# Preparing the attention's weights behind the norms instead of at the head of the expert walk

## The chip, the cores and the metric

The kernel runs on one core of a Trainium2 chip. A core has a TensorE (PE, matmul; its weight loads are listed as PEld), a VectorE (DVE), a ScalarE (ACT), a GpSimd (POOL) and a SyncE (SP, which here issues DMAs). Each engine works through its own list of instructions in order; engines wait for each other by semaphores. The metric is the time of one execution on the device in microseconds (us). The clock times below count from the start of the profiled span.

## The reference

The input x has 2 x 1024 rows of 256. Every row is normalized; the result xn goes to two branches whose outputs are added to x.

```
xn = layernorm(x)
out = x + attention(xn) + moe(xn)

attention: tokens of 16 channels (each row of 256 holds 16 of them), on a grid of 256 x 64
  q, k, v = tok @ qkv_w
  two branches of 8 channels: softmax attention inside windows of 8 tokens (1 x 8 and 8 x 1),
  plus a depthwise 3 x 3 convolution of v with its bias
  att = concat(branches) @ proj_w + proj_b
  tok + layernorm(att) * ln_w + ln_b

moe: 16 experts with 176 hidden units, plus a shared expert with 352
  scores = sigmoid(xn @ gate.T); of 4 groups of experts the best 2, of those the best 6 experts
  out = sum over the chosen experts of weight * (silu(xn @ gate_e.T) * (xn @ up_e.T)) @ down_e.T
        + shared expert
```

A convolution over a window that is one token wide uses only three of the nine taps, so the whole path from xn to the convolution's share of the attention output is linear. The kernel folds it into small matrices once per call.

## The kernel before

**Norms.** x lies in 128 partitions, 16 rows in each, as four groups of four. `statistics(g)` and `normalized(g)` make means, scales and normalized rows of a group; PE transposes them (L244) into xnT, copied out by ACT (L247) and DVE (L249). `logits(g)` makes the routing's logits (L255, L260).

**Shared expert.** `meanwhile(until)` lays steps of the shared expert between the other work by a budget: products pg and pu (L273), Silu on ACT (L281), the gated product on DVE (L282, tile room), the down product py (L288), the copy to ysh (L289), and after each group of four an accumulating store of ysh to the output, issued by POOL (L291).

**Routing.** From L343 to L538 DVE finds groups, experts and ranks, sorts the 2048 rows by expert sets into 16 tiles of 128, and makes the lists. Its scratch tile tmp holds eight pieces of 128 x 256.

**Walk.** `sorted_tile(t)` gathers a tile's rows (POOL, L817, three buffers), transposes them (px, L821), copies them (xsT, L822) and their weights (wsrt, L824). For each tile three units of two experts follow, and some extra units. `begun` makes the up products pr_u (L853), Silu (L855) and hms on DVE (L856); `hidden` transposes hms (ph, L867) and copies (hT, L869); `finished` makes the down products pr_y (L879) and gives the sum to a scatter that adds into the output (L994). Over the slots the planner lays steps of the attention: `while step and done[0] <= pace * done[1]`, where done sums up estimated costs of DVE and PE and pace comes from in_walk, the estimated costs of all steps. Other small jobs (`extras_listed` at L546, `lists_begun` at L900) are laid into fixed slots.

**Attention.** Four heads (two halves of the batch, two halves of the row). `project(i)` makes pq (L671) from wq and copies q, k and v on ACT (L673 to L676), `products` and `scores` (L684, L688), `highest` (L694 to L696), `weighted` and `values` (L705, L710), `divide` (L718), and `transposed` (L725, L727) into oT. At the end `attended` (L761) adds the projection wp and the folded convolution lp with the bias pbc (pp, L777), normalizes, and the result is stored by accumulation.

**The part that is moved.** `weights_prepared` makes wq, wp, lp and pbc from the weights that DMAs brought at the start. Its steps are qp8 (L583), pqp and qprep (L586, L588), wq (L592), the centring of prep and pb (L598 to L600), wp, rd and wvr (L605 to L612), pm, pb and mm (L615 to L621), ppb and pbc (L626 to L628), and lp (L633 to L642). Before, `all_steps` yields eight of these, each with an estimate of 1.0 for DVE and 0.1 for PE, ahead of the attention's steps.

What decides the final order: a scheduling layer takes the kernel's recorded instructions and lays them out engine by engine; it may move an instruction ahead of others that were recorded earlier where its inputs allow. In the profiled kernel qp8 and the two wvr copies run at 18.6 to 21.8 us, among the norms.

Buffers that tie these parts together: the tag qk holds the routing's tmp and later the attention's q and k; ysum and ysh share the tag ysum; the two PSUM buffers of ps_m (tag m) serve the transposes of the norms, pqp, pm, ppb, px, pq and po; the tag xd holds qp8, wvr, pb8, part and pair_i (two buffers).

Of the kernel before, what the change touches and what calls it, by code (L numbers as in the profile page):

```python
# [8 lines left out]
F32 = mybir.dt.float32  # L9
# [4 lines left out]
ALU = mybir.AluOpType  # L14
AX = mybir.AxisListType
# [7 lines left out]
P = 128  # L23
B, H, W = 2, 1024, 256
C = 16
# [26 lines left out]
def csw_block_moe(ctx: ExitStack, tc: tile.TileContext, x, qkv_w, conv_w0, conv_b0, conv_w1, conv_b1,  # L52
# [58 lines left out]
    ident = const.tile([P, P], F32, name="ident")  # L111
# [89 lines left out]
    cbc = const.tile([C, 1], F32, name="cbc")  # L201
# [4 lines left out]
    band = const.tile([P, 3, 8], F32, name="band")  # L206
# [108 lines left out]
    def meanwhile(until):  # L315

        while spent[1] is not None and spent[0] + spent[1] <= until:
            spent[0] += spent[1]
            spent[1] = next(share)

    held = statistics(0)
    for g in range(4):
        now, held = held, statistics(g + 1) if g < 3 else None
        normalized(g, *now)
        if g > 0:
            logits(g - 1)
        meanwhile((0, 3.4, 6.8, 6.8)[g])
    table_of(AF.Sigmoid, xnT[:, 0, 15, P - 1 : P])
    logits(3)

# [124 lines left out]
    for c in range(15, -1, -1):  # L455
# [3 lines left out]
        to = beats[:, 0:n].rearrange("p c q -> p (c q)")  # L459
# [33 lines left out]
    for n in range(2):  # L493
        nc.vector.tensor_tensor(ohp[:, 8 * n : 8 * n + 8], row_h.unsqueeze(1).to_broadcast(wide),
                                place[:, 1, 8 * n : 8 * n + 8].unsqueeze(2).to_broadcast(wide), ALU.is_equal)
        for c in range(8 * n, 8 * n + 8):
# [38 lines left out]
                     start=True, stop=True)  # L535
# [10 lines left out]
    def extras_listed():  # L546
# [24 lines left out]
        nc.vector.tensor_scalar(xrow[:, 1], xrow[:, 1], NX, None, op0=ALU.add)  # L571
        nc.vector.tensor_scalar(xrow[:, 2], xrow[:, 2], 4, None, op0=ALU.logical_shift_right)
        yield


    def weights_prepared():

        qp8 = work.tile([4 * C, 8, C], F32, tag="xd", name="qp8", bufs=2)
        nc.vector.tensor_copy(qp8, qpT.unsqueeze(1).to_broadcast([4 * C, 8, C]))  # L583
        yield
        pqp = ps_m.tile([P, 4 * C], F32, tag="m", name="pqp")
        nc.tensor.transpose(pqp, qp8.rearrange("k t c -> k (t c)"), ident[0 : 4 * C, 0 : 4 * C])  # L586
        qprep = const.tile([P, 4 * C], F32, name="qprep")
        nc.vector.tensor_copy(qprep, pqp)  # L588
        yield
        qrep, prep = qprep[:, 0 : 3 * C], qprep[:, 3 * C : 4 * C]  # L590
        for s in range(3):
            nc.vector.tensor_tensor(wq[:, s], qrep[:, C * s : C * s + C].unsqueeze(1).to_broadcast([P, 8, C]),  # L592
                                    band[:, 0, :].unsqueeze(2).to_broadcast([P, 8, C]), ALU.mult)
        yield

        def centred(v):
            m = small.tile([P, 1], F32, tag="cm", name="cm")
            nc.vector.tensor_reduce(out=m, in_=v, axis=AX.X, op=ALU.add)  # L598
            nc.vector.tensor_scalar(m, m, 1.0 / C, None, op0=ALU.mult)
            nc.vector.tensor_scalar(v, v, m, None, op0=ALU.subtract)  # L600

        centred(prep)
        centred(pb)
        yield
        nc.vector.tensor_tensor(wp, prep.unsqueeze(1).to_broadcast([P, 8, C]),  # L605
                                band[:, 0, :].unsqueeze(2).to_broadcast([P, 8, C]), ALU.mult)
        rd = const.tile([C, 5, C], F32, name="rd")
        nc.vector.tensor_tensor(rd, prep[0:C, :].unsqueeze(1).to_broadcast([C, 5, C]),
                                tp.unsqueeze(2).to_broadcast([C, 5, C]), ALU.mult)
        wvr = work.tile([C, 2, 8, C], F32, tag="xd", name="wvr", bufs=2)  # L610
        nc.vector.tensor_copy(wvr[:, 0], wvT.unsqueeze(1).to_broadcast([C, 8, C]))
        nc.vector.tensor_copy(wvr[:, 1].rearrange("p t c -> p (t c)"), cbc.to_broadcast([C, P]))  # L612
        yield
        pm = ps_m.tile([P, 6, C], F32, tag="m", name="pm")
        nc.tensor.matmul(pm[:, 0:5, :].rearrange("p d c -> p (d c)"), lhsT=wvr[:, 0].rearrange("p t c -> p (t c)"),  # L615
                         rhs=rd.rearrange("p d c -> p (d c)"), start=True, stop=True)
        nc.tensor.matmul(pm[:, 5, :], lhsT=wvr[:, 1].rearrange("p t c -> p (t c)"), rhs=prep[0:C, :], start=True,
                         stop=True)
        nc.vector.tensor_tensor(pb, pb, pm[:, 5, :], ALU.add)
        mm = const.tile([P, 5, C], F32, name="mm")  # L620
        nc.vector.tensor_copy(mm, pm[:, 0:5, :])  # L621
        yield

        ppb = ps_m.tile([P, P], F32, tag="m", name="ppb")
        pb8 = work.tile([P, 8, C], F32, tag="xd", name="pb8", bufs=2)
        nc.vector.tensor_copy(pb8, pb.unsqueeze(1).to_broadcast([P, 8, C]))  # L626
        nc.tensor.transpose(ppb, pb8.rearrange("p t c -> p (t c)"), ident)
        nc.vector.tensor_copy(pbc, ppb[:, 0:1])  # L628
        yield
        part = work.tile([P, 2, 8, C], F32, tag="xd", name="part", bufs=2)  # L630

        def banded(to, tap, d):
            nc.vector.tensor_tensor(to, mm[:, tap, :].unsqueeze(1).to_broadcast([P, 8, C]),  # L633
                                    band[:, d, :].unsqueeze(2).to_broadcast([P, 8, C]), ALU.mult)

        banded(lp[:, 0], 1, 0)
        banded(part[:, 0], 0, 1)
        banded(part[:, 1], 2, 2)
        banded(lp[:, 1], 3, 0)
        banded(lp[:, 2], 4, 0)  # L640
        nc.vector.tensor_tensor(lp[:, 0], lp[:, 0], part[:, 0], ALU.add)
        nc.vector.tensor_tensor(lp[:, 0], lp[:, 0], part[:, 1], ALU.add)  # L642
        yield

    wq = const.tile([P, 3, 8, C], F32, name="wq")
    wp = const.tile([P, 8, C], F32, name="wp")
    lp = const.tile([P, 3, 8, C], F32, name="lp")
    pbc = const.tile([P, 1], F32, name="pbc")


    oT = big.tile([P, 4, 2, 4, P], F32, name="oT", tag="oT")
# [392 lines left out]

    att = []

    def all_steps():
        for _ in weights_prepared():
            yield 1.0, 0.1, lambda: None
        yield from attention_steps()  # L1050

    def attention_steps():
        for b in range(B):
            for h in range(2):
                yield from attention(b, h)
# [16 lines left out]
    of_slot = {"six": (0.5, 2.0), "extra": (0.8, 2.5)}  # L1072
    of_tile = (0.75, 0.25)
    END = 72
    in_walk = [8 * 1.0 + 4 * (16 * 2.3 + 3.3 + 2.5 + 1.5 + 1.4) + 0.6 + 8 * 1.4, 8 * 0.1 + 4 * 6.2 + 8 * 3.9]
    done = [0.0, 0.0]
    whole = [in_walk[n] + NTL * TOPK * of_slot["six"][n] + NL * of_slot["extra"][n] + NTL * of_tile[n] for n in range(2)]
    pace = (whole[0] - END * of_slot["six"][0] / of_slot["six"][1]) / (whole[1] - END)
# [1 line left out]
    def counted(cost):  # L1080
        for n in range(2):
            done[n] += cost[n]

    walk = all_steps()
    sorted_tile(0)
    meanwhile(100)
    sorted_tile(1)
# [50 lines left out]
    with tc.For_i(0, count_, 1) as n:  # L1138
# [3 lines left out]
        to = small.tile([P, 1], I32, tag="to", name="to")  # L1142
# [60 lines left out]
```

## Time and profile before

| what | value |
|---|---|
| median of 3 runs | 447.4 us (447.02 to 449.18) |
| profiled execution | 447.97 us |
| its span, first to last instruction | 446.3 us |
| mean granted clock of TensorE | 0.987 |
| qprep (L588) of the preparation | 102.15 us |
| last addition of lp (L642) | 111.79 us |
| first product of the attention (L684) | 119.05 us |
| landing of a ysh store, shortest, median, longest | 5.4, 5.6, 7.9 us |

The profile lists, for an instruction or a group, its start, its duration, and in brackets the idle time of its engine just before it with what ended that idle time. A wait for several semaphores is put down to the one that came last by the profile. The chain of waits follows the end back to the start, step by step to what released each.

### The profile page before, as it was taken

Reading aid. Unit: us, or ns where it says so; the run is one execution under the profiler, and the core shown is the slowest. Engines: PE = TensorE matmul, PEld = TensorE weight load, DVE = VectorE, ACT = ScalarE, POOL = GpSimd, SP = SyncE. Lnnn points to the kernel's source line nnn. Section 1 sums busy time; section 2 is a strip of 40 time slices with the busy share of each in tenths; the row PEclk is TensorE's granted clock in tenths of the full one; section 3 lists DMA queues with packets and bytes.
Section 4 is the critical chain, followed back from the end, with each engine's and each line's share of the span. In section 5 each row is a group of like instructions: output and inputs, shape, how many; then the busy total and the mean of one; then the engine's idle time right before and its main releaser. Section 6 shows DMA issues by size and latency. Waiting matters only on the chain.

```text
span 446.3 us, 6293 instructions
## 1 busy us (share of the span) xinstructions
PE 393.4 (88%) x1668; PEld 246.3 (55%) x1669; DVE 291.5 (65%) x515; ACT 214.1 (48%) x535; POOL 197.9 (44%) x207
## 2 busy tenths in 40 slices
PE   0999999997899788998897999999998899979990
PEld 0435465664466555565564666656665555446670
DVE  4624958635699979289995999959999223322210
ACT  2945258322544442643635456364533657774320
POOL 7300000314273299457524245615554274779432
PEclk9999999999999999999999999999999999998997
DMA  8999941324023101101212124210332101822922
GB/s 232 338 304 321 275 154 30 64 67 86 25 71 73 32 25 34 29 23 33 38 39 60 35 43 81 47 36 24 69 90 56 22 14 57 103 68 74 126 44 24
DMA packets 40178, 37.56 MB, mean 84 GB/s; under 512 B 5300, under 2 KB 37616, under 8 KB 40112
## 3 DMA queue, kind: packets, MB, share of 16 engines
q0 software_dynamic: 11616, 13.52, 18.4%
q1 hardware_dynamic: 27472, 22.59, 16.4%
q10 hardware_dynamic: 1056, 1.05, 0.7%
q8 instruction: 15, 0.25, 0.2%
q14 instruction: 19, 0.16, 0.1%
HBM read 27.70 MB, written 12.45 MB: 90 GB/s over the span
## 4 chain that ended last, share of the span: by engine, by line
DVE 38%; PE 30%; DMA 10%; issue 8%; ACT 7%; POOL 5%; DVEq 0%; POOLq 0%; ACTq 0%; SPq 0%
DVE s L688 6%; PE pr_u L853 6%; DVE pv L705 6%; DVE pr L684 5%; DVE o L710 5%; DVE hms L856 5%; PE pp L777 4%; PE pq L671 3%; PE pr_y L879 3%; DMA out_dram<-ysum,lists 3%; PE pg L273 3%; PE py L288 2%; DMA xg<-xw_d,lists 2%; PE pu L273 2%; DMA xx<-in_x_dram 2%
## 5 line engine op out<-in xcount | busy, mean ns | idle before, releaser
L853 PE MATMUL pr_u<-w1s,xsT 128*128 x384 | 128.4, 468 | 3.4 <-DVE hms L856 2.4
L853 PEld LDWEIGHTS pr_u<-w1s,xsT 128*128 128x128 f32 x384 | 69.9, 191 | 39.4 <-issue 7.7
L994 POOL DMA_INDIRECT out_dram<-ysum,lists x30 | 57.2, 1908 | 77.4 <-ACT ysum L1040 20.3
L855 ACT ACTIVATE sg<-pr_u 128x176 f32<-128x176 f32 x110 | 34.7, 317 | 77.1 <-PE pr_u L853 70.2
L856 DVE SCALAR_TENSOR_TENSOR hms<-sg,w,pr_u 128x176 f32<-128x176 f32 x96 | 36.8, 387 | 35.5 <-ACT sg L855 35.5
L684 DVE TENSOR_TENSOR pr<-qk 128x2048 f32<-128x2048 f32 x16 | 36.6, 2288 | 17.6 <-ACT qk L673 17.2
L705 DVE TENSOR_TENSOR pv<-s,v 128x2048 f32<-128x2048 f32 x16 | 36.5, 2284 | 2.5 <-ACT s L696 2.4
L867 PE MATMUL ph<-ident,hms 128*128 128x128 f32 x165 | 31.7, 282 | 5.5 <-DVE hms L856 2.9
L688 DVE TENSOR_REDUCE s<-pr 128x256 f32<-128x2048 f32 x16 | 36.5, 2279 | 0.1
L955 POOL TENSOR_SCALAR ysum<-row_h,spot 128x128 f16<-128x128 f16 x26 | 28.0, 1094 | 19.2 <-PE rows_of L946 14.9
L710 DVE TENSOR_REDUCE o<-pv 128x256 f32<-128x2048 f32 x16 | 36.3, 2269 | 0.0
L980 POOL DMA_INDIRECT xg<-xw_d,lists x14 | 21.6, 1540 | 29.3 <-DVE hms L856 15.5
L867 PEld LDWEIGHTS ph<-ident,hms 128*128 128x128 f32 x165 | 21.5, 144 | 23.2 <-DVE hms L856 6.9
L291 POOL DMA_DIRECT2D out_dram<-ysh x4 | 3.7, 928 | 64.5 <-ACT ysh L289 64.5
L817 POOL DMA_INDIRECT xg<-xw_d,lists x16 | 19.8, 1239 | 25.4 <-PE ph L867 9.3
L879 PE MATMUL pr_y<-w2a,hT 128*128 x96 | 29.1, 386 | 0.0
L879 PE MATMUL pr_y<-wts,hT 128*128 128x256 f32 x96 | 29.0, 384 | 0.0
L879 PE MATMUL pr_y<-w2b,hT 112*128 x96 | 28.8, 381 | 0.0
L671 PE MATMUL pq<-wq,rows 128*128 128x384 f32 x64 | 25.1, 506 | 3.3 <-ACT oT L727 1.9
L869 ACT COPY hT<-ph 128x384 f32<-128x384 f32 x55 | 26.4, 480 | 2.8 <-PE ph L867 1.8
L853 PE MATMUL pr_u<-w1s,xd 128*128 x56 | 20.4, 487 | 6.6 <-ACT xd L989 6.6
L288 PE MATMUL py<-room 128*128 128x256 f32 x96 | 23.9, 387 | 0.7 <-DVE room L282 0.7
(403 smaller groups left out, 712.2 us busy)
## 6 DMA issues: line engine op xcount, KB each, us to landing
w1s<-in_w_dram SPq DMA_DIRECT2D x22, 256.0 KB, 4.4
wts<-in_w_dram SPq DMA_DIRECT2D x55, 64.0 KB, 2.1
wts<-in_w_dram SPq DMA_DIRECT2D x55, 48.0 KB, 1.7
xw_d<-xx SPq DMA_DIRECT2D x4, 544.0 KB, 4.6
w2a<-in_w_dram SPq DMA_DIRECT2D x4, 512.0 KB, 9.4
out_dram<-ysh POOLq DMA_DIRECT2D x4, 512.0 KB, 5.6
xr<-xw_d POOLq DMA_DIRECT2D x4, 512.0 KB, 5.0
out_dram<-att POOLq DMA_DIRECT2D x8, 256.0 KB, 6.4
```

Of the source, the lines that this page charges most:

```text
L288: nc.tensor.matmul(py, lhsT=hms[k, m][:, P * c : P * c + P], rhs=w2h[:, m], start=(m == 0), stop=(m == 2))
L671: nc.tensor.matmul(pq.rearrange("p s t c -> p (s t c)"), lhsT=rows[:, i], rhs=wq.rearrange("p s t c -> p (s t c)"), start=True, stop=True)
L684: nc.vector.tensor_tensor(pr, q_.unsqueeze(3).to_broadcast(full), k_.unsqueeze(2).to_broadcast(full), ALU.mult)
L688: nc.vector.tensor_reduce(out=s[:, n : n + NW], in_=held.pop(n), axis=AX.X, op=ALU.add)
L705: nc.vector.tensor_tensor(pr, s[:, n : n + NW].unsqueeze(3).to_broadcast(full), v[:, br, m : m + NW].unsqueeze(2).to_broadcast(full), ALU. ...
L710: nc.vector.tensor_reduce(out=o[:, n : n + NW], in_=held.pop(n), axis=AX.X, op=ALU.add)
L853: nc.tensor.matmul(pu, lhsT=lhs[:, h, :], rhs=w1s[:, :, h, bass.ds(e * I, I)], start=(h == 0), stop=(h == 1))
L855: nc.scalar.activation(sg, pu[:, 0, :], AF.Silu)
L856: nc.vector.scalar_tensor_tensor(hm[:, 0:I], sg, w, pu[:, 1, :], op0=ALU.mult, op1=ALU.mult)
L867: nc.tensor.transpose(ph[:, s, :], units[:, P * s : P * s + P], ident)
L879: nc.tensor.matmul(py, lhsT=l_, rhs=r_, start=start and n == 0, stop=stop and n == 2)
L994: nc.gpsimd.indirect_dma_start(out=out_rows, out_offset=bass.IndirectOffsetOnAxis(ap=index, axis=0), in_=ys, in_offset=None, bounds_check= ...
```

## The change

The definition of `weights_prepared`, with its four result tiles, moves up to stand before the loop over the norms' groups. It is run through at once behind the loop, before the Sigmoid table and the last logits. The attention's steps then start the walk alone, and the estimates of the eight steps leave in_walk. The body of the function is unchanged.

```diff
@@ before the loop over the norms' groups
+    wq = const.tile([P, 3, 8, C], F32, name="wq")
+    wp = const.tile([P, 8, C], F32, name="wp")
+    lp = const.tile([P, 3, 8, C], F32, name="lp")
+    pbc = const.tile([P, 1], F32, name="pbc")
+
+    def weights_prepared():
...
     held = statistics(0)
     for g in range(4):
         now, held = held, statistics(g + 1) if g < 3 else None
...
         if g > 0:
             logits(g - 1)
         meanwhile((0, 3.4, 6.8, 6.8)[g])
+    for _ in weights_prepared():
+        pass
     table_of(AF.Sigmoid, xnT[:, 0, 15, P - 1 : P])
     logits(3)
...
-    def weights_prepared():
...
-    wq = const.tile([P, 3, 8, C], F32, name="wq")
-    wp = const.tile([P, 8, C], F32, name="wp")
-    lp = const.tile([P, 3, 8, C], F32, name="lp")
-    pbc = const.tile([P, 1], F32, name="pbc")
...
-    def all_steps():
-        for _ in weights_prepared():
-            yield 1.0, 0.1, lambda: None
-        yield from attention_steps()
-
...
-    in_walk = [8 * 1.0 + 4 * (16 * 2.3 + 3.3 + 2.5 + 1.5 + 1.4) + 0.6 + 8 * 1.4, 8 * 0.1 + 4 * 6.2 + 8 * 3.9]
+    in_walk = [4 * (16 * 2.3 + 3.3 + 2.5 + 1.5 + 1.4) + 0.6 + 8 * 1.4, 4 * 6.2 + 8 * 3.9]
...
-    walk = all_steps()
+    walk = attention_steps()
```

The order of the instructions per engine changes with it: 23 VectorE instructions and the four matmuls of the preparation leave the head of the walk and stand between the last transposes of the norms and the routing. On POOL the iota of pair_i (L555) moves from the walk to a place ahead of the first ysh store, and its cast (L556) into the routing on VectorE. SP's order is the same.

More of the change, by code (lines that the diff above doesn't have):

```diff
@@ L319, in meanwhile, with centred, banded @@
             spent[1] = next(share)
+    wq = const.tile([P, 3, 8, C], F32, name="wq")
[3 more added lines that the diff above has]
+    def weights_prepared():
+        qp8 = work.tile([4 * C, 8, C], F32, tag="xd", name="qp8", bufs=2)
+        nc.vector.tensor_copy(qp8, qpT.unsqueeze(1).to_broadcast([4 * C, 8, C]))
+        yield
+        pqp = ps_m.tile([P, 4 * C], F32, tag="m", name="pqp")
+        nc.tensor.transpose(pqp, qp8.rearrange("k t c -> k (t c)"), ident[0 : 4 * C, 0 : 4 * C])
+        qprep = const.tile([P, 4 * C], F32, name="qprep")
+        nc.vector.tensor_copy(qprep, pqp)
+        yield
+        qrep, prep = qprep[:, 0 : 3 * C], qprep[:, 3 * C : 4 * C]
+        for s in range(3):
+            nc.vector.tensor_tensor(wq[:, s], qrep[:, C * s : C * s + C].unsqueeze(1).to_broadcast([P, 8, C]),
+                                    band[:, 0, :].unsqueeze(2).to_broadcast([P, 8, C]), ALU.mult)
+        yield
+        def centred(v):
+            m = small.tile([P, 1], F32, tag="cm", name="cm")
+            nc.vector.tensor_reduce(out=m, in_=v, axis=AX.X, op=ALU.add)
+            nc.vector.tensor_scalar(m, m, 1.0 / C, None, op0=ALU.mult)
+            nc.vector.tensor_scalar(v, v, m, None, op0=ALU.subtract)
+        centred(prep)
+        centred(pb)
+        yield
+        nc.vector.tensor_tensor(wp, prep.unsqueeze(1).to_broadcast([P, 8, C]),
+                                band[:, 0, :].unsqueeze(2).to_broadcast([P, 8, C]), ALU.mult)
+        rd = const.tile([C, 5, C], F32, name="rd")
+        nc.vector.tensor_tensor(rd, prep[0:C, :].unsqueeze(1).to_broadcast([C, 5, C]),
+                                tp.unsqueeze(2).to_broadcast([C, 5, C]), ALU.mult)
+        wvr = work.tile([C, 2, 8, C], F32, tag="xd", name="wvr", bufs=2)
+        nc.vector.tensor_copy(wvr[:, 0], wvT.unsqueeze(1).to_broadcast([C, 8, C]))
+        nc.vector.tensor_copy(wvr[:, 1].rearrange("p t c -> p (t c)"), cbc.to_broadcast([C, P]))
+        yield
+        pm = ps_m.tile([P, 6, C], F32, tag="m", name="pm")
+        nc.tensor.matmul(pm[:, 0:5, :].rearrange("p d c -> p (d c)"), lhsT=wvr[:, 0].rearrange("p t c -> p (t c)"),
+                         rhs=rd.rearrange("p d c -> p (d c)"), start=True, stop=True)
+        nc.tensor.matmul(pm[:, 5, :], lhsT=wvr[:, 1].rearrange("p t c -> p (t c)"), rhs=prep[0:C, :], start=True,
+                         stop=True)
+        nc.vector.tensor_tensor(pb, pb, pm[:, 5, :], ALU.add)
+        mm = const.tile([P, 5, C], F32, name="mm")
+        nc.vector.tensor_copy(mm, pm[:, 0:5, :])
+        yield
+        ppb = ps_m.tile([P, P], F32, tag="m", name="ppb")
+        pb8 = work.tile([P, 8, C], F32, tag="xd", name="pb8", bufs=2)
+        nc.vector.tensor_copy(pb8, pb.unsqueeze(1).to_broadcast([P, 8, C]))
+        nc.tensor.transpose(ppb, pb8.rearrange("p t c -> p (t c)"), ident)
+        nc.vector.tensor_copy(pbc, ppb[:, 0:1])
+        yield
+        part = work.tile([P, 2, 8, C], F32, tag="xd", name="part", bufs=2)
+        def banded(to, tap, d):
+            nc.vector.tensor_tensor(to, mm[:, tap, :].unsqueeze(1).to_broadcast([P, 8, C]),
+                                    band[:, d, :].unsqueeze(2).to_broadcast([P, 8, C]), ALU.mult)
+        banded(lp[:, 0], 1, 0)
+        banded(part[:, 0], 0, 1)
+        banded(part[:, 1], 2, 2)
+        banded(lp[:, 1], 3, 0)
+        banded(lp[:, 2], 4, 0)
+        nc.vector.tensor_tensor(lp[:, 0], lp[:, 0], part[:, 0], ALU.add)
+        nc.vector.tensor_tensor(lp[:, 0], lp[:, 0], part[:, 1], ALU.add)
+        yield
@@ L573, in extras_listed @@
         yield
-    def weights_prepared():
[L582 to L643, printed above, removed]
```

## The prediction

> **What bounds the kernel now.** I read the page's busy times and the chain first, then the table of stretches by time, then the timelines of the two places the edit touches.
>
> ```profile
> PE 393.4 (88%) x1668; PEld 246.3 (55%) x1669; DVE 291.5 (65%) x515; ACT 214.1 (48%) x535; POOL 197.9 (44%) x207
> ...
> DVE 38%; PE 30%; DMA 10%; issue 8%; ACT 7%; POOL 5%; DVEq 0%; POOLq 0%; ACTq 0%; SPq 0%
> ```
>
> TensorE is the busiest, yet the chain runs more often through VectorE. The stretches say where:
>
> ```profile
> 20.00:30.00 10.00, 10.00 (x36) 4.25 (x36) 1.50 (x3) 5.17 (x9) 0.00 (x0) 1.00 0.99 290
> 30.00:40.00 10.00, 10.00 (x37) 4.17 (x36) 2.05 (x3) 6.59 (x9) 0.00 (x0) 1.00 1.12 346
> ...
> 200.00:210.00 10.00, 8.85 (x40) 5.84 (x39) 10.00 (x9) 2.83 (x12) 7.95 (x9) 1.00 0.20 36
> ```
>
> Columns: length, busy PE, PEld, DVE, ACT, POOL, granted clock, DMA. Under the norms (20 to 40) PE is full and DVE nearly empty. Inside an attention head DVE is full and PE has gaps. The timeline of the first place:
>
> ```profile
> 30.90 0.69 DVE L249 COPY xnT<-pt 128x512 f32<-128x512 f32 x1
> 39.33 0.69 DVE L282 TENSOR_TENSOR room<-room,pu 128x512 f32<-128x512 f32 x1 [7.74 <-PE pu L273]
> 40.21 0.43 DVE L345 TENSOR_TENSOR tmp<-tmp,ebias 128x256 f32<-128x256 f32 x1 [0.19 <-ACT tmp L343]
> ```
>
> Between the last copy of the norms and the routing's first operation VectorE is idle for 7.74 us. The second place, the head of the walk:
>
> ```profile
> 107.62 0.42 DVE L551 SCALAR_TENSOR_TENSOR ysum<-tmp,extras 128x256 bf16<-128x256 f32 x1 [2.52 <-DMA xg<-xw_d,lists]
> 110.23 0.45 PE L627 MATMUL ppb<-ident,pb 128*128 128x128 f32 x1 [2.76 <-DVE pb L626]
> 111.96 2.05 PE L853 MATMUL pr_u<-w1s,xsT 128*128 x4
> 116.38 0.27 ACT L673 COPY qk<-pq 128x128 f32<-128x128 f32 x1 [2.02 <-DVE xnum L562]
> 119.05 2.29 DVE L684 TENSOR_TENSOR pr<-qk 128x2048 f32<-128x2048 f32 x1 [1.72 <-ACT qk L673]
> ```
>
> L551 writes into the buffer that the shared experts' result ysh also occupies, so what it really waits for is not the gather that is named but the last ysh store (issued at 101.95; POOL's L933, which waits for the same store, starts at 107.54). Behind L551 stand the preparation's second half (L619 to L642) and an hms; PE waits at ppb. The attention's first product starts at 119.05.
>
> **The change part by part.** The order of the changed kernel's instructions shows that 23 of the preparation's 26 VectorE instructions move. The other three (qp8 and two wvr copies) stood among the norms already, at 18.6 to 21.8, as did all its DMAs; no DMA is moved, and SP's queue stays as it was.
>
> *Removed at the head of the walk.* VectorE, by distances of starts: qprep 0.22, three wq and two sums 0.76, the centring to rd 0.84, pb to the last lp 1.44, two additions 0.40: 3.66 us. PE: pqp 0.21, pm 0.29 and 0.33, ppb 0.24: 1.07 us. The waits: 0.41 before the up product at 106.02 and 2.76 at ppb.
>
> *Added behind the norms.* On PE pqp comes behind the logits' product at 32.6, so qprep can start at 32.8 and rd is done 1.82 later, at 34.7; PE reaches pm at 36.1, so it does not wait. pm 0.6, half of pg 0.93, ppb at 37.65 (pb8 ready at 37.1), done at 37.9. VectorE ends at about 38.9, inside its 7.74 us. So the 3.66 us are covered; uncovered they would stand on the routing. PE has no cover: its 1.07 us push pu, so room (L282) starts at 40.4 instead of 39.33 and the routing at 41.0 instead of 40.21. ACT's two table loads there (1.28 each) come only 0.21 later and stay ahead of that. Farther on, the cast of pair_i (0.20 start to start) slips into the routing. PE has lost 0.40 and 0.34 us in waits for VectorE at 56.1 and 96.4, both following the same shift, so the walk begins about 0.95 late. The 1.07 PE us are thus moved, not saved.
>
> *Moved past.* POOL's iota of pair_i goes from 110.76 to just behind ppb, far ahead of the first ysh store at 46.94: free. But POOL's memset (L933) now stands ahead of the gather of tile 5, behind the last ysh store; before, two gathers preceded it.
>
> *The opening of the walk after.* wq is ready, so two pq run after the first up product. Four ups (1.28 each) and two pq (0.66 each) fill PE from 101.5 to 108.0. The next step (ph) needs the second hms, still behind the ysh wait: store at 102.9, landing 5.54 later at 108.45, then L551, L907, L552, L560 and hms: 109.9. PE is idle 1.9. Then ph, 0.33. The next pq needs a PSUM buffer, which ACT frees only once it may write qk, whose room is the routing's tmp, until the last L562: seven VectorE steps, 2.0, to 111.95; four copies 0.7. PE is idle again, 2.4. Together 4.3, against 0.41 + 2.76 + 1.27 (at 117.16) = 4.4 before: **PE gains nothing here**, the wait changes its name. VectorE does: the first four qk are copied at 115.3 to 116.1, and the product starts about 3.0 us before 119.05.
>
> *A rule to weigh: the clock.* The table of stretches across the idle:
>
> ```profile
> 108.00:110.00 2.00, 0.00 (x0) 0.00 (x0) 2.00 (x11) 0.00 (x0) 0.00 (x0) 0.99 0.00 0
> 110.00:112.00 2.00, 1.77 (x9) 1.80 (x10) 2.00 (x12) 0.59 (x2) 0.90 (x2) 0.50 0.04 8
> 112.00:114.00 2.00, 2.00 (x6) 1.29 (x6) 1.41 (x7) 0.58 (x2) 1.70 (x2) 0.66 0.06 11
> ```
>
> 2.76 us of idle cost half the clock for about 3.1 us (the up product at 111.96 takes 2.05 instead of 1.35), some 1.5 us of work. The Trainium skill (TensorE: Matmul & The Clock Gate, Part 1) says that PE drops to half after at least one idle window of about 3.4 us. By that rule neither idle of 1.9 or 2.4 would throttle, and the change would save 1.5 us more; by the row it throttles again. I take the row: 0.33 us of work between two idles is hardly a recovery.
>
> *Gathers.* Tiles 5, 6 and 7 reuse buffers that PE now frees only after the eight pq (about 119 instead of 102.5 for the first). POOL issues them about 1.27 apart, landing takes 2.8 to 3.0, and their transposes stand close together in PE's order: about 0, 0.6 and 1.1 us of wait. Bounds 0 and 3; I take 1.9, but while VectorE is the later engine this does not reach the end.
>
> *The rest.* By count of hms, the four heads' first products stand at 5, 29, 49, 69 before and at 4, 26, 47, 68 after; the last head's last values (L710) at 86 and 85, and the final attended steps at 88 to 96 in both. The pace that the code computes falls from 1.182 to 1.149. Heads keep about their length; a gap of three slots moves from behind head one to behind head three. So one more slot must be run in the stretch that starts 3.0 us earlier: 0.31 (one hms) if VectorE bounds it, about 2.1 (up, half of ph and pr_y) if PE does. Gain 2.7 or 0.9; since VectorE is at 9 to 10 of 10 inside heads but PE at the boundaries, I take 2.0.
>
> **The sum.** Span 446.3 - 2.0 = 444.3; the profiled run took 447.97, 1.67 beyond its span, so 445.97 in its terms. It was 0.57 above the median of the runs, so against that: 447.4 - 2.0 = **445.4**. About 0.5% (2.2 us) is what a measurement of this kernel can tell from no change.
>
> **The rivals.**
>
> *The lead is carried through.* Head two starts three slots (6 us of PE) earlier. If VectorE fills all the rest, PE's idle of 13 us between 200 and 350 absorbs the extra slots, and 3 to 6 are gained: about 443. For it: the full DVE windows. Against: the gap behind head three, where VectorE waits for the planner's slots.
>
> *Slower: the gathers hold PE.* Place: the tile transposes between the sixth and the fifteenth up product. A gather needs a buffer whose weights VectorE has copied out (wsrt) and whose rows PE has turned. Before, nine of the sixteen were issued ahead of the first attention product (the last at 113.56); now five are, and the copies for the others stand between products and sums of 2.2 each, while PE, in order, waits at the transposes. Price: 1.9 at tiles 5 to 7, and for the eight behind them up to the 0.7 that my ledger gives for tile 9 (buffer free at 128.5, landing 131.7, PE there at 131.0): 0 to 7.5 in all, taken at 3. If PE is then the later engine the lead is worth nothing: about +3, 450.5. It decides once PE reaches the tenth up product's end (133.3 before) later than about 134. For it: by my ledger PE ends it level, but with 0.9 us of transposes and of px still to come. Against: in the profile PE loses only 0.3 to 0.4 at such a place, and VectorE is the fuller engine.
>
> *Nothing.* The preparation stood largely in the shadow of the ysh store that both versions await at 107.5 to 108.5, and the two boundaries that are PE's eat the lead: 447, within 1.2 either way.
>
> That the change does not do what it says is excluded by the order, apart from the three copies.
>
> **How the numbers follow.** The forecast has 0.37 (444.3 to 446.8; a third of it beyond 0.5%), the carried lead 0.24 (nearly all beyond), nothing 0.15, slower 0.24 (nearly all beyond). Faster by over 0.5%: 0.13 + 0.24 = 0.37; slower 0.23; the rest 0.40. The forecast's own range is 444.3 to 446.8; the range for 8 in 10 reaches from the carried lead to most of the slower case, 442.0 to 451.0.
>
> **What would show it.** Right: DVE's idle of 7.74 between 31.6 and 39.3 is mostly filled, the routing starts at about 41; no ppb near 110; PE idle about 1.9 and 2.4 behind the fourth up product; the first attention product at 115 to 117; the last attended step some 2 us earlier than before. Wrong: room or tmp waits for a preparation step; the first product comes at 118 or later; waits of PE for gathers over 2 us in sum; the attended steps begin no earlier although the products did, which would make PE the bound of the heads.

## The result and the profile after

The changed kernel takes 463.25 us (median of 4 runs, 460.9 to 464.56) against 447.75 us before (4 runs, 447.02 to 449.18): 1.032 times, 95% interval 1.027 to 1.037. The forecast of 445.4 was wrong, and 463.25 lies outside its range for 8 in 10 (442.0 to 451.0). The profiled execution took 464.56, its span is 462.8 us (16.5 longer than before), at a mean granted clock of 0.965 against 0.987.

The page's busy row and the engines of the chain, to set beside those of before:

```profile
PE 400.0 (86%) x1668; PEld 250.1 (54%) x1669; DVE 292.2 (63%) x515; ACT 214.4 (46%) x535; POOL 188.3 (41%) x207
...
PE 36%; DVE 24%; DMA 15%; issue 10%; POOL 8%; ACT 5%; POOLq 0%; SPq 0%; DVEq 0%; ACTq 0%
```

The numbers of instructions are the same. TensorE is busy 6.6 us longer with the same 1668 matmuls, and 9.9 us more it is idle. In the chain VectorE's share has fallen from 38% to 24%, while TensorE (30 to 36%), DMA (10 to 15%) and GpSimd (5 to 8%) have gained: the end now hangs more on TensorE, on transfers and on GpSimd.

The front, in the timeline of VectorE (start, duration, in brackets the idle time before it):

```profile
32.41 0.22 DVE L339 COPY qprep<-pqp 128x64 f32<-128x64 f32 x1 [1.33 <-PE pqp L337]
...
38.13 0.29 DVE L393 TENSOR_TENSOR lp<-lp,part 128x128 f32<-128x128 f32 x1
39.67 0.69 DVE L282 TENSOR_TENSOR room<-room,pu 128x512 f32<-128x512 f32 x1 [1.25 <-PE pu L273]
40.28 0.42 DVE L422 TENSOR_TENSOR tmp<-tmp,ebias 128x256 f32<-128x256 f32 x1
```

The whole preparation lies in what was an idle of 7.74 us, and the routing begins at 40.28 instead of 40.21. The front costs next to nothing: the walk's first hms is 0.43 us late.

The opening of the walk, from the timeline:

```profile
108.10 0.42 DVE L628 SCALAR_TENSOR_TENSOR ysum<-tmp,extras 128x256 bf16<-128x256 f32 x1 [3.63 <-DMA out_dram<-ysh]
109.78 0.44 PE L869 MATMUL ph<-ident,hms 128*128 128x128 f32 x2 [2.42 <-DVE hms L858]
112.81 2.93 PE L673 MATMUL pq<-wq,rows 128*128 128x384 f32 x4 [2.59 <-ACT v L678]
116.07 2.29 DVE L686 TENSOR_TENSOR pr<-qk 128x2048 f32<-128x2048 f32 x1 [2.15 <-ACT qk L675]
```

This too is what was forecast: the wait for the ysh store, which the profile now names, the two idles of TensorE, half the clock behind them (four matmuls of pq take 2.93 us; four at full clock 1.45 at 198.74), and a first attention product 2.98 us earlier. The clock was still 1.00 at 110 to 112 us, behind the first idle; behind the second it was 0.65 and then 0.50 (112 to 116 us). Up to here nothing is lost that counts. What follows is new. First the gathers, whose transposes stand in TensorE's order (timeline of TensorE):

```profile
126.01 0.41 PE L823 MATMUL px__1181<-ident,xg 128*128 128x128 f32 x2 [1.47 <-DMA xg<-xw_d,lists]
127.29 0.41 PE L823 MATMUL px__1208<-ident,xg 128*128 128x128 f32 x2 [0.87 <-DMA xg<-xw_d,lists]
138.35 0.41 PE L823 MATMUL px__1306<-ident,xg 128*128 128x128 f32 x2 [1.66 <-DMA xg<-xw_d,lists]
145.49 0.41 PE L823 MATMUL px__1375<-ident,xg 128*128 128x128 f32 x2 [2.48 <-DMA xg<-xw_d,lists]
```

These are tiles 6, 7, 11 and 14. The waits sum to 6.48 us; before there was one, at tile 9:

```profile
126.31 0.41 PE L821 MATMUL px__1239<-ident,xg 128*128 128x128 f32 x2 [0.32 <-DMA xg<-xw_d,lists]
```

Then the lists of pairs, which L955 to L958 build from 26 "spots" (ScalarE copies a 128 x 3 tile, GpSimd makes two tiles of zeros and ones from it, TensorE multiplies them into rows_of, L948). They need the weights of all sixteen gathered tiles, so they start later. The first line is the step of the lists in the kernel before, the others are of the changed kernel:

```profile
154.68 0.27 DVE L931 TENSOR_SCALAR ysum<-ysum 128x256 int32<-128x256 int32 x1
...
166.15 0.29 DVE L933 TENSOR_SCALAR ysum<-ysum 128x256 int32<-128x256 int32 x1
166.35 0.40 DVE L858 SCALAR_TENSOR_TENSOR hms<-sg,w,pr_u 128x176 f32<-128x176 f32 x1
...
169.37 2.29 DVE L707 TENSOR_TENSOR pv<-s,v 128x2048 f32<-128x2048 f32 x1
169.61 2.38 POOL L958 TENSOR_SCALAR ysum<-row_h,spot 128x26 f16<-128x26 f16 x1
...
172.04 0.18 PE L948 MATMUL rows_of<-ysum 128*128 128x26 f16 x1 [2.77 <-POOL ysum L958]
172.55 2.71 PE L855 MATMUL pr_u<-w1s,xsT 128*128 x4 [0.32 <-issue]
...
176.55 0.40 DVE L858 SCALAR_TENSOR_TENSOR hms<-sg,w,pr_u 128x176 f32<-128x176 f32 x1 [4.89 <-ACT sg L857]
```

TensorE waits for a spot, the clock halves (the up product takes 2.71 instead of 1.35), and VectorE then waits 4.89 us for a Silu (before, 2.50 us for one behind the spots). The chain of the changed kernel passes through all of this: the landings for tiles 11 and 14 (4.91 us from 133.30 and 3.09 us from 142.27), the up product behind the second (2.54 us at 147.75), the spot at 169.61 and the up products of 172.55 and 175.12.

The table of stretches of the changed kernel (length, busy PE, PEld, DVE, ACT, POOL, granted clock, DMA share, GB/s) shows the two worst places, this one and the boundary behind head one:

```profile
170.00:180.00 10.00, 7.64 (x23) 4.78 (x23) 5.11 (x5) 2.55 (x10) 7.55 (x12) 0.66 0.01 3
...
190.00:200.00 10.00, 9.21 (x25) 5.43 (x26) 1.91 (x5) 5.45 (x23) 1.05 (x2) 0.66 0.01 4
```

In the kernel before the clock is 1.00 in both:

```profile
170.00:180.00 10.00, 8.50 (x39) 5.75 (x38) 8.59 (x10) 2.39 (x10) 9.07 (x11) 1.00 0.19 38
...
190.00:200.00 10.00, 10.00 (x45) 6.76 (x45) 8.49 (x8) 4.01 (x21) 6.24 (x8) 1.00 0.09 25
```

At the boundary TensorE is idle for 1.92 and then 0.68 us, works at half the clock from 192 to 198 us (0.50 to 0.52 granted), and VectorE waits 8.06 us for the first q and k of head two. Before, TensorE's wait there is 0.69 us, and VectorE's 4.79.

To place the loss I set the two series of hms side by side (L856 before, L858 after, by number). The lag of the changed kernel is 0.4 us at the first, 1.8 at the 10th, 6.5 at the 13th, 11.3 at the 24th, 15.9 at the 34th, and 16.5 at the 45th; the span ends 16.5 longer. Nearly all of it arises between 135 and 220 us, and at most 0.4 us where the preparation now stands.

### The profile page after: what moved, and what is told of

It reads as the page before. It is cut to its first block, busy times and chain, and to the rows that moved or that the text cites. A ratio compares the mean times of both kernels' runs of the same rounds, so it can differ in the third digit from the quotient of the medians.

```text
span 462.8 us, 6291 instructions
## 1 busy us (share of the span) xinstructions
PE 400.0 (86%) x1668; PEld 250.1 (54%) x1669; DVE 292.2 (63%) x515; ACT 214.4 (46%) x535; POOL 188.3 (41%) x207
## 4 chain that ended last, share of the span: by engine, by line
PE 36%; DVE 24%; DMA 15%; issue 10%; POOL 8%; ACT 5%; POOLq 0%; SPq 0%; DVEq 0%; ACTq 0%
PE pr_u L855 8%; DVE pv L707 5%; DVE o L712 4%; PE pg L273 4%; DVE s L690 4%; DMA xg<-xw_d,lists 4%; PE pp L779 4%; PE py L288 4%; DMA out_dram<-att 4%; DMA out_dram<-ysum,lists 4%; PE pr_y L881 3%; PE pu L273 3%; DVE pr L686 3%; PE pq L673 3%; DVE hms L858 3%
## 5 line engine op out<-in xcount | busy, mean ns | idle before, releaser
L855 PE MATMUL pr_u<-w1s,xsT 128*128 x384 | 132.3, 478 | 1.4 <-DVE hms L858 0.7
L855 PEld LDWEIGHTS pr_u<-w1s,xsT 128*128 128x128 f32 x384 | 72.1, 196 | 42.2 <-issue 12.2
L996 POOL DMA_INDIRECT out_dram<-ysum,lists x30 | 50.9, 1697 | 80.8 <-ACT ysum L1035 21.8
L858 DVE SCALAR_TENSOR_TENSOR hms<-sg,w,pr_u 128x176 f32<-128x176 f32 x96 | 36.9, 390 | 49.7 <-ACT sg L857 46.8
L869 PE MATMUL ph<-ident,hms 128*128 128x128 f32 x165 | 30.7, 279 | 9.7 <-DVE hms L858 6.0
L957 POOL TENSOR_SCALAR ysum<-row_h,spot 128x128 f16<-128x128 f16 x26 | 24.4, 960 | 31.0 <-PE rows_of L948 12.1
L673 PE MATMUL pq<-wq,rows 128*128 128x384 f32 x64 | 28.3, 566 | 5.1 <-ACT v L678 2.9
L273 PE MATMUL pg<-xnT,room 128*128 128x512 f32 x48 | 24.0, 612 | 0.0
```

The costliest lines, as they stand in the source:

```text
L273: nc.tensor.matmul(ps, lhsT=w1h[:, half, h, P * m : P * m + P], rhs=xnT[:, h, 4 * k : 4 * k + 4, :].rearrange("p l q -> p (l q)"), start=( ...
L673: nc.tensor.matmul(pq.rearrange("p s t c -> p (s t c)"), lhsT=rows[:, i], rhs=wq.rearrange("p s t c -> p (s t c)"), start=True, stop=True)
L855: nc.tensor.matmul(pu, lhsT=lhs[:, h, :], rhs=w1s[:, :, h, bass.ds(e * I, I)], start=(h == 0), stop=(h == 1))
L858: nc.vector.scalar_tensor_tensor(hm[:, 0:I], sg, w, pu[:, 1, :], op0=ALU.mult, op1=ALU.mult)
L869: nc.tensor.transpose(ph[:, s, :], units[:, P * s : P * s + P], ident)
L996: nc.gpsimd.indirect_dma_start(out=out_rows, out_offset=bass.IndirectOffsetOnAxis(ap=index, axis=0), in_=ys, in_offset=None, bounds_check= ...
```

## The experiments

Every kernel ran beside the kernel before. The first figure is its median; the ratio is to the kernel before, with its 95% interval in brackets. The expectation, in a quotation, stands ahead of the result.

The theories. **A**: the place of the preparation costs nothing; the loss comes from the slots of the walk that its eight steps gave up, so that attention begins earlier in the walk. **B**: the preparation ahead of the routing costs. **C**: the lower pace does it. **D, E, F** name what follows from the slots: D the late gathers, E the small tile spot, F GpSimd's chain of spots.

**1. Two crossed kernels: place against slots.** The spacers keep the preparation in front and put eight empty steps into the walk:

```diff
+    def all_steps():
+        for _ in range(8):
+            yield 1.0, 0.1, lambda: None
+        yield from attention_steps()
-    in_walk = [4 * (16 * 2.3 + ...
+    in_walk = [8 * 1.0 + 4 * (16 * 2.3 + ...
-    walk = attention_steps()
+    walk = all_steps()
```

> The preparation stays behind the norms, but the walk begins with eight empty steps at the old estimates (1.0 and 0.1) and the old sum in in_walk, so that every attention step falls into the slot it had before (first products at hms 5, 29, 49, 69 as before). Theory A, the loss comes from the slots that the eight dropped steps give up, not from where the preparation runs: the loss of 15.5 us vanishes, 444 to 448. Theory B, the preparation ahead of the routing itself costs: it stays near 463. A share of both would lie between; I expect 446.

The counterpart starts from the kernel before and gives its eight steps no weight (`yield 0.0, 0.0, ...`, and the changed in_walk).

> The counterpart of the spacers, made from the kernel before: the preparation stays at the head of the walk, but its eight steps are given estimates of zero and leave in_walk, so that the attention's steps fall into nearly the changed kernel's slots (first products at hms 5, 27, 47, 68). Theory A (slots): it is slower than before like the changed kernel, 458 to 465. Theory B (place of the preparation): it stays at 447 to 449. I expect 460.

Measured: spacers 449.17 us, 1.0009 (0.999 to 1.0027); the counterpart 469.2, 1.0421 (1.0368 to 1.0474). A holds and B falls: with the old slots the loss is gone, with the new slots it is there although the preparation never moved. At the new slots the moved preparation comes out no worse (1.032 against 1.0421; the two intervals just touch, and the slots are nearly but not quite the same).

**2. The pace alone.** The changed kernel with the old in_walk.

> The changed kernel with the old sum in in_walk, so the pace is 1.182 as before, not 1.149; attention still begins at hms 4. The later heads then begin at hms 26, 45, 65. Theory C, the lower pace spreads the steps over more slots and that costs the 15.5 us: it falls back to about 448 to 451. Theory A with the opening as the cause (attention's first steps ahead of the tiles' gathers): it stays at 458 to 466. I expect 460.

It took 462.88 us, 1.0307 (1.0269 to 1.0344), which cannot be told from 1.032. C falls: heads two to four at hms 26, 45, 65 are as bad as at 26, 47, 68.

**3. The gathers.** Four buffers instead of three:

```diff
-        xg = work.tile([P, ROW], F32, tag="xg", name="xg", bufs=3)
+        xg = work.tile([P, ROW], F32, tag="xg", name="xg", bufs=4)
-        sums = small.tile([P, 16, WIN], F32, name=f"sums{b}{h}", tag="sums")
+        sums = small.tile([P, 16, WIN], F32, name=f"sums{b}{h}", tag="sums", bufs=1)
```

> The changed kernel with four gather buffers instead of three (the room comes from the tag sums, one buffer instead of two). Nothing else differs. Theory D, late gathers hold TensorE and what follows at 168 to 200 us is only their consequence: most of the 15.5 us return, 448 to 452. If the gathers cost only what their four waits show (1.47 + 0.87 + 1.66 + 2.48, and a stretch at half clock behind the last): 4 to 7 us return, 456 to 459. If the gathers do not matter: 463. I expect 457.

It took 455.29 us, 1.0121 (1.0076 to 1.0167): some 8 us return, more than the 6.48 of waits. D has a large part, with what it drags along. The single buffer of sums is no hidden price: VectorE alone writes and reads that tile, in its own order.

Which engine holds the buffers? The weights of a tile are copied out by VectorE (wsrt, L826); a kernel gives that copy to ScalarE.

```diff
-        nc.vector.tensor_copy(w, xg[:, W:ROW])
+        nc.scalar.copy(w, xg[:, W:ROW])
```

> The changed kernel with the copy of a tile's weights (wsrt, L826) on ScalarE instead of VectorE, so that a gather's buffer no longer waits for a place between two attention products on VectorE. If VectorE's release is what makes the gathers late: TensorE's waits at px (1.47, 0.87, 1.66, 2.48 us) nearly go, and it comes to 453 to 457, like four buffers. If TensorE's own order holds the buffers: 461 to 464. I expect 457.

It took 466.51 us, 1.035 (1.0283 to 1.0417): no gain, and outside both ranges that were expected. TensorE's waits for tiles 11 and 14 (1.66 and 2.48) are gone, but tiles 5 to 7 wait (1.76, 0.72 and 0.50), and now ScalarE waits for landings (timeline of that kernel):

```profile
128.26 0.20 ACT L826 COPY wsrt<-xg 128x16 f32<-128x16 f32 x1 [1.99 <-DMA xg<-xw_d,lists]
128.37 0.41 PE L823 MATMUL px__1139<-ident,xg 128*128 128x128 f32 x2 [1.76 <-DMA xg<-xw_d,lists]
```

The other side: hold back the attention for four slots, so that tiles 2 to 7 stand in TensorE's order nearly as they did (before: behind 1, 2, 4, 4, 6, 6 up products; here 1, 2, 3, 4, 6, 6; in the changed kernel behind 5 to 6, with the pq of head one ahead of or among them).

```diff
-            while step and done[0] <= pace * done[1]:
+            while step and i >= 4 and done[0] <= pace * done[1]:
```

> The changed kernel with one condition more: no attention step is laid in the first four slots. In TensorE's order the transposes of tiles 2 to 7 then stand behind 1, 2, 3, 4, 6 and 6 up products again, as before (in the changed kernel: 5 to 6, because eight pq stand ahead of them); the later heads keep the changed kernel's slots (26, 47, 68) and its pace. Theory A narrowed to the opening: the eight pq ahead of the tiles are the whole cause, 447 to 451. If the other slots of heads two and three are a cause of their own: 454 or more. I expect 450.

It took 459.78 us, 1.0207 (1.0148 to 1.0265): a part returns, about 5 us by the ratios. The expectation of 450 was wrong. The gathers are still late, now by VectorE (timeline of this kernel):

```profile
124.17 0.96 POOL L819 DMA_INDIRECT xg<-xw_d,lists  x1 [0.30 <-PE pr_u L855]
...
129.74 2.29 DVE L686 TENSOR_TENSOR pr<-qk 128x2048 f32<-128x2048 f32 x1
131.94 0.17 DVE L826 COPY wsrt<-xg 128x16 f32<-128x16 f32 x1
132.86 1.01 POOL L819 DMA_INDIRECT xg<-xw_d,lists  x1 [7.73 <-DVE hms L858]
135.81 0.41 PE L823 MATMUL px__1364<-ident,xg 128*128 128x128 f32 x2 [2.03 <-DMA xg<-xw_d,lists]
```

The copy of tile 10's weights stands behind an attention product of 2.29 us, and the gather of tile 13, which takes over its buffer, goes out only once VectorE has passed that place, after 7.73 us of idle on GpSimd (the profile names the hms that follows the copy). TensorE then waits 2.03 us for it. So the early attention holds the buffers twice: on TensorE by pq, on VectorE by its products. A cure on one side alone left waits on the other.

> Four gather buffers and the hold of four slots together, in the changed kernel. In TensorE's order tiles 2 to 15 then stand as with the spacers; the later heads keep slots 26, 47, 68. If late gathers, by whichever release, are the whole loss: 447 to 451. If the slots of the later heads cost by themselves: 453 to 456. The two alone gave 455.3 and 459.8. I expect 451.

With both (hold and four buffers): 456.3 us, 1.0173 (1.0119 to 1.0226). The gathers now cost one wait of 1.67, and still nothing is gained over four buffers alone (1.0121). The expectation of 451 was wrong: late gathers are not the whole.

**4. The spots.** First the small tile: four buffers of spot, in the changed kernel, with four gather buffers, and in the kernel before.

```diff
-        spot = small.tile([P, 3], F32, name="spot", tag="spot")
+        spot = small.tile([P, 3], F32, name="spot", tag="spot", bufs=4)
```

> The changed kernel with four buffers of the small tile spot (128 x 3) instead of two, so that a copy of a spot on ScalarE (L955) no longer waits for GpSimd's work on the spot two before it. Theory E, the list building is the second place of loss: ScalarE's copies, each waiting about a microsecond for GpSimd, stand ahead of the Silu that TensorE and VectorE need (VectorE waited 4.89 us for it). Then some 4 to 6 us return: 457 to 459. If GpSimd's own pace of about 1.05 us a spot is what TensorE waits for (rows_of stands in TensorE's order), nothing returns: 462 to 464. I expect 459.

> Four gather buffers and four spot buffers together in the changed kernel. Four gather buffers alone gave 455.3. If gathers and list building are two losses that add, 450 to 452, near the kernel before; if four spot buffers free nothing, 455. I expect 452.

> The kernel before with four spot buffers. There VectorE waited 2.50 us for a Silu behind the spots. Theory E says that a little is to be had here too, 445 to 448 (1 to 3 us); if GpSimd's pace decides, 449 as before. I expect 447.

The changed kernel took 467.51 us, 1.0422 (1.0382 to 1.0463); with four gather buffers 455.63, 1.0137 (1.0101 to 1.0174); the kernel before 452.07, 1.0061 (1.0037 to 1.0086). None is faster than without the four buffers of spot. E falls: the wait that the profile named at ScalarE was not the bound, since rows_of waits for GpSimd as before (again 1.07 and 2.77 us in the first of the three). And the tile is not neutral: with it, the kernel before lags by 0.4 us at the 45th hms and by 3.5 at the 49th, so something later was laid in another way; what it is stays open. A candidate made with it:

> The candidate: preparation behind the norms, eight empty steps in its place, four gather buffers and four spot buffers. The trace of the spacers alone led the kernel before by 3.6 to 4.4 us from the 7th to the 19th hms and lost all of it at 155 to 162 us, where five copies of spots stood ahead of one Silu (VectorE waited 5.22 us). If the four spot buffers keep the lead: 444 to 446, faster than both kernels. If the next head boundary, where VectorE waits for the planner's slots and TensorE is full, takes it anyway: 448 to 449. I expect 446.

It took 452.53 us, 1.0066 (1.0038 to 1.0094): slower than the spacers alone, and outside both ranges.

Then GpSimd's work itself: its second operation on each spot (L958) goes to VectorE.

```diff
-        nc.gpsimd.tensor_scalar(spots[:, P:], row_h[:, 0:NX], ...
+        nc.vector.tensor_scalar(spots[:, P:], row_h[:, 0:NX], ...
```

> The changed kernel with the second of the two operations on each spot (L958, 128 x 26) on VectorE instead of GpSimd. Theory F: from the moment the spots can start, GpSimd's chain of 26 spots at about 1.05 us paces TensorE (the lag at hms 34 follows the start of the spots in every kernel so far: spots 1.2 us earlier, 7.3 and 11.5 us later went with +0.1, +7.2 and +15.9). With 0.46 us off each spot the chain shortens by up to 12 us, and 4 to 8 us return: 455 to 459. If the lag only rides on the late start and TensorE would catch nothing up: 461 to 465. I expect 458.

> The kernel with spacers (preparation behind the norms, old slots) with L958 on VectorE. It led the kernel before by 4 us until the spots began. Theory F: the chain of spots took that lead, and with a shorter chain it is kept, 444 to 446, better than both kernels. If the boundary behind the first head is set by the planner's slots and not by the spots: 448 to 450. I expect 446.

The changed kernel with it took 455.96 us, 1.0127 (1.0086 to 1.0169). F holds there: 7 us return although the step of the lists (L933) comes 12.8 us late. The edit also keeps the second operation from standing beside VectorE's products on GpSimd (last section), so a shorter chain and fewer collisions are not told apart. The spacers with it took 452.59, 1.0072 (1.0045 to 1.01), slower than both expectations. By hms, though, the lead over before, which the spacers alone had lost by the 24th hms, lasted (4.5 us at the 24th, 3.5 at the 37th). It was lost by the 49th, 3.5 us late, in a stretch where late spots stand between VectorE's products. So the edit was cut to the first 16 spots:

```diff
+        (nc.vector if n < 16 else nc.gpsimd).tensor_scalar(spots[:, P:], ...
```

> The spacers with L958 on VectorE for the first 16 spots only. With all 26 on VectorE the lead of 3.6 us over the kernel before lasted to the 37th hms and was lost at 215 to 240 us, where spots on VectorE stood between products and held rows_of. With the late spots on GpSimd again the lead should last: 444 to 447, faster than both kernels. If the planner's slots take it at the next boundary: 448 to 450. I expect 446.

> The spacers with 16 spots on VectorE again, unchanged, for a narrower interval and beside the kernel before with the same edit. 443 to 446; ratio to before 0.986 to 0.993.

> The kernel before with L958 of the first 16 spots on VectorE; the preparation stays in the walk. If the spots alone make the gain of the spacers with the same edit (444.4): 443 to 446. If the moved preparation's lead of 3.6 us at the opening is what is now kept: 447 to 449, and the other 444. In the kernel before, TensorE and VectorE waited little for the spots (2.50 us once), so I expect 447.

The spacers with it took 444.39 us, 0.9895 (0.9865 to 0.9925), and again 444.26, 0.9903 (0.9878 to 0.9928): about 1% faster than the kernel before, beyond the interval. The kernel before with it took 447.48, 0.9965 (0.9947 to 0.9983). The page of the spacers with 16 spots:

```profile
PE 392.0 (89%) x1668; PEld 245.7 (56%) x1669; DVE 295.8 (67%) x531; ACT 214.4 (49%) x535; POOL 186.8 (42%) x191
PEclk9999999999999999999998999999999999998997
```

VectorE does 16 operations more, and TensorE's clock (in tenths, by slices of the span) keeps its nines in the first 21 slices, where the changed kernel lost them from the 13th on. The intervals of 0.9903 and 0.9965 do not overlap: the preparation in front is worth about 3 us, if the slots are the old ones and the spots do not take the lead.

**5. What the slots cost by themselves.** Two cures together, then all three, in the changed kernel:

> Four gather buffers, and the second operation on the first 16 spots on VectorE, in the changed kernel. Alone the first gave 455.3 and the second, for all 26 spots, 456.0. Separate losses: 447 to 451. One chain, of which either cures the same part: 453 to 456. I expect 450.

> The changed kernel with the hold of four slots, four gather buffers and the first 16 spots on VectorE. If the three delays are the whole loss: 444 to 449, and the lag of hms 34 behind before is about 0 or below. If the lower pace costs by itself, because head two begins after 26 hms instead of 29 and TensorE, which ends last from there on, has three slots more still to do: 451 to 455 and a lag of 3 to 6 at hms 34. I expect 452.

With two cures it took 454.89 us, 1.0114 (1.0069 to 1.0159), with all three 454.27, 1.0115 (1.0074 to 1.0155). The cures don't add: four buffers alone gave 1.0121, shorter spots alone 1.0127. As I read it, they work on one chain (early attention, late gathers, late lists, TensorE held by the spots, half clock), and each takes most of it away. About 1.1% stays, 5 us, that no cure touched and that only the old slots removed. The last kernel's time is the one expected for a price of the slots themselves, but its lag at the 34th hms is 1.8 us, between the two expectations (about 0, and 3 to 6).

How that rest comes about, in the kernel with all three cures: its 24th hms is 1.6 us earlier than before and head two's first product 4.0 us earlier, yet its 45th hms is 4.6 us late and the span is 6.2 longer. Head two begins there after 26 hms, not 29. Head one ran beside fewer up products, and TensorE has three slots more left. Whether the 5 us are the three slots' own work alone is not settled.

Against their nearest kernels with the old slots the price is larger. The kernel with all three cures has the tiles' transposes in TensorE's order just as the spacers with 16 spots have them (tiles 2 to 15 behind 1, 2, 3, 4, 6, 6, 6, 7, 8, 9, 10, 11, 11 and 12 up products), and the same spots; it differs in the attention's slots and in the fourth gather buffer. It takes 1.0115 against 0.9903, some 10 us more. The hold with four gather buffers, set beside the plain spacers in the same way, takes 1.0173 against 1.0009, some 7 us more. So the slots cost much even where the gathers stand in their old order.

The lags in us behind the kernel before, by number of hms, from the profiled executions (a minus means ahead):

| kernel, hms: | 14th | 24th | 34th | span |
|---|---|---|---|---|
| changed | 9.7 | 11.3 | 15.9 | 16.5 |
| spacers | -2.6 | 0.1 | 0.1 | 1.2 |
| four gather buffers | 5.2 | 7.0 | 7.1 | 9.6 |
| hold of four slots | 5.6 | 6.3 | 10.9 | 11.5 |
| L958 on VectorE | 11.0 | 5.1 | 7.1 | 9.0 |
| hold, buffers and 16 spots | 4.2 | -1.6 | 1.8 | 6.2 |
| spacers, 16 spots | -3.5 | -6.2 | -6.7 | -5.5 |

In none of the kernels run here was a lag at the 34th hms made up afterwards; the span's difference lies 0.6 us or more above it. That TensorE's work in order decides from there on is my reading; it was not tested.

## Why the prediction was wrong

*What was right.* **The front**: the 3.66 us of VectorE lie in the idle, the routing begins 0.07 us later (0.8 had been charged) and the walk 0.43 (0.95 had been charged). **The opening**: idles of 2.42 and 2.59 us (1.9 and 2.4 forecast), first product at 116.07 (about 3.0 us earlier, 2.98 measured). **The clock**: taking the row of before was right against the rule of the Trainium skill (TensorE: Matmul & The Clock Gate, Part 1), half the clock after an idle window of about 3.4 us: neither idle was that long, and half the clock followed the second. The row was used for the opening only, though. The later idles throttled too (0.84 of the clock at 140 to 150 us, 0.66 at 170 to 180 and at 190 to 200, against 1.00 in each before), and the sum had no term for them. They are, as I read it, the 6.6 us of extra busy time: the matmuls are the same in number, and the stretches at half clock are where they took longer.

*The step that failed first: "Gathers".* It took 1.9 us of waits at tiles 5 to 7 (its own three figures add up to 1.7) and stopped with "while VectorE is the later engine this does not reach the end". There the waits were 0, 1.47 and 0.87, near the estimate (0, 0.6, 1.1). The two large ones, 1.66 and 2.48, came at tiles 11 and 14, which the sum left at zero. They did reach the end: four gather buffers brought some 8 us back. The way was twofold: at TensorE directly, and by the lists, whose start (the step of L933 on VectorE; L931 before) came at 166.15 instead of 154.68. The lists are not named in the prediction at all, although GpSimd was busy 9.5 of 10 us at 160 to 170 in the table of before.

*The step that failed next: "The rest".* It carried 2.0 of the 3.0 us of the earlier first product to the end and priced the heads' new places (hms 26, 47 and 68) at one slot more, because VectorE is full inside heads. The kernel with all three cures has a lead of 4.0 us at head two and ends 1.15% slower than before, and 2.1% slower than the spacers with 16 spots, which have the old slots. As I read it, an attention step that is earlier in the order of hms gains nothing if TensorE is then behind by hms: VectorE's heads and TensorE's tail are paid one after the other, and the up products that head one no longer covers are left over. How this part of the loss arises stays open.

*The rivals.* The slower rival named the right place, the right two releases (wsrt and the transposes), and the right test: TensorE's tenth up product ended at 134.9, later than the 134 from which it was to decide. Its own waits summed to 6.48 within its bounds of 0 to 7.5, against the 3 taken. What was mis-sized is what hangs behind: it ended the count at the transposes and came to 450.5, some 13 us short. "The lead is carried through" is refuted in the changed kernel, and realized only with the old slots and shorter spots. "Nothing" describes the spacers.

## What to carry to other kernels

Taking steps out of a planned order also moves all that stood behind them: cost the move of the neighbours as a change of its own, and try it with empty steps in the old places, which tells the two apart in one run. Look for small jobs in fixed slots that need the last of a series (here the lists, which need sixteen gathers) and for the engine that then runs them at its own pace. A copy of 0.17 us that frees a buffer is as late as the instruction of 2.29 us in front of it.

## What the runs showed of the hardware

GpSimd's 128 x 26 operation took 0.46 us, but 2.38 when VectorE's pv, a product of two inputs over 128 x 2048 elements, ran at the same time (169.61 and 169.37 in the timeline above), and both ended within 0.4 us of each other. In the kernel before, the 128 x 26 operation took 2.46 us from 166.74, beside a pv from 166.58; beside VectorE's o, a sum over one tile, GpSimd kept 0.61 (128 x 128) and 0.47 us (128 x 26):

```profile
156.47 2.27 DVE L710 TENSOR_REDUCE o<-pv 128x256 f32<-128x2048 f32 x1
156.54 0.61 POOL L955 TENSOR_SCALAR ysum<-row_h,spot 128x128 f16<-128x128 f16 x1 [2.63 <-DVE hms L856]
157.15 0.47 POOL L956 TENSOR_SCALAR ysum<-row_h,spot 128x26 f16<-128x26 f16 x1
```

The Trainium skill (SBUF — State Buffer, "SBUF: two separate sides") says that a VectorE operation with two inputs in SBUF and a GpSimd operation that reads SBUF exclude each other for a whole instruction; the trace agrees. It makes GpSimd's chain of spots depend on where the attention's products stand. The collisions are not new with the change: eight of the 52 spot operations took over 2 us before, six after. What is new is that TensorE waited for one of them (2.77 us at 172.04).

The clock fell to half again without a single idle as long as the 3.4 us named above: in the changed kernel TensorE was idle for 1.07 and 2.77 us around a matmul of 0.17 us, and the clock stayed at 0.50 over 172 to 176 us:

```profile
168.00:170.00 2.00, 0.20 (x2) 0.19 (x2) 2.00 (x3) 0.39 (x2) 2.00 (x4) 1.00 0.19 50
170.00:172.00 2.00, 0.00 (x0) 0.00 (x0) 1.65 (x1) 0.00 (x0) 2.00 (x2) 0.66 0.02 7
172.00:174.00 2.00, 1.64 (x4) 0.96 (x4) 0.00 (x0) 0.39 (x2) 2.00 (x4) 0.50 0.00 0
174.00:176.00 2.00, 2.00 (x6) 1.06 (x5) 0.00 (x0) 0.39 (x2) 2.00 (x5) 0.50 0.00 0
```

The last two rows show the price: TensorE is busy for 1.64 and 2.00 of 2 us, at half the pace.
